# Four-layer scan network on one core: operand offsets, nine units of B on GpSimd placed by turn, Silus in the second turn, the line layer's addition one scan later

## The chip, the cores and the metric

The kernel runs on one NeuronCore of a Trainium2 chip. The metric is the time of one execution on the device, in microseconds (us). A core has five engines that run their own instruction streams and meet at semaphores: PE (TensorE, matrix products), DVE (VectorE), ACT (ScalarE), POOL (GpSimd) and SP, which here does nothing but issue DMAs. SBUF is the on-chip memory of 128 partitions, PSUM the smaller memory that PE writes and that DVE and ACT can read; DRAM tiles hold what is sent around.

## The reference, cut to what matters

Eight images of 48 x 48 pixels and 96 channels go through four residual layers, `x = x + layer(group_norm(x))`. Layers 0 and 3 are "SS2D" layers, layer 1 is a spectral layer (up-sampling, a small multi-layer product, low-pass), layer 2 is a line layer. Layers 0, 2 and 3 are selective scans. With u the convolved and Silu-activated input of 192 channels, 16 states and 4 directions:

```
xz = x @ in_proj;  u, z = split(xz);  u = silu(conv(u) + b)      # 3x3 in SS2D, 4 taps along the line in layer 2
x_dbl = u (in direction k) @ x_proj                              # -> dt (rank 6), B (16), C (16)
delta = softplus(dt @ dt_proj + bias)                            # one value per channel and pixel
for every pixel in the direction's order:
    h = h * exp(delta * A) + (delta * u) * B                     # h: 192 channels x 16 states
    y = sum over states of h * C
y = y + D * u
# SS2D: sum of the 4 directions over the whole image, layer norm, * silu(z), @ out_proj
# line layer: every row (or column) is its own sequence; * silu(z), @ outp, the directions joined by @ out_w
```

In SS2D one sequence runs through all 2304 pixels; in the line layer h starts anew in every row or column of 48 pixels.

## The kernel before, in words

**Tiling.** `scans` is the common body of layers 0, 2 and 3. A layer has 8 jobs (images) of 4 directions of 5 blocks: four blocks of 10 lines (480 columns) and one of 8 (384), 160 blocks in all. The 192 channels are two halves of 96, the 16 states and 96 channels of a half are folded into four groups of 128 partitions x 3 units. So a block has 8 slots (half and group, in the order of `ORDER`), each of three units of one block's columns, and four turns q of two slots (six units) each. A turn does, per pair of units, one scan on DVE (line 289) over both units at once. In the SS layers a unit has two more columns than the block (`m = n + 2`): at one side the state that came from the block before with `FAR` as its delta, at the other one that is multiplied by nothing; in the line layer `m = n`, and `FAR` is put on the first pixel of every line.

**What a turn computes, and where.** `make_da` (line 281): exp(delta * A) on ACT into one of two PSUM buffers, two exponentials for each scan. `make_dbu` (line 257): du * B into a room in SBUF, a part of the three units of a slot on DVE, with B from a PSUM copy that ACT makes (`copy_b`, line 238, one buffer), the rest on POOL, with B straight from the SBUF tile `bc`; `ON_POOL` says how many units of which slot are POOL's: seven in a block. `scan` runs in place in the room. `make_hc` (line 295): h * C on POOL, in place, eight times a block. `reduce` (lines 315, 317): sums over states on PE into PSUM, after an `opening` product that brings in what is summed so far (line 311). `done`: in SS a copy of y by ACT into the sum (line 671), in the line layer y * silu(z) on DVE (line 822), then two later steps, `project` on PE at +1 (line 831) and `add` on DVE at +2 (lines 837 and 839).

**What sets the order.** The schedule is by hand (`manual_schedule`): each engine runs its instructions in program order. The order within a turn t is that of the loop at line 368: scan(t,0); hc of the turn before; DVE's part of slot 2t+2; exponentials for the next scan; POOL's part of slot 2t+3; a reduction; scan(t,1); and so on. `aside` is called twice a turn, once a slot, and holds what stands beside the scans: the loads of B and C (`LOAD_BC`, slots 2, 3, 6, 7) and of delta and du (`LOAD_DD`, slots 4 and 5) for the next block, one step of the `side` generator, the steps of `stage1`, the `later` steps of `done`, and the `tail`.

**Stage 1** prepares block b + 2 while block b is scanned. In SS: slot 0 the product with x_proj on PE (line 630), slot 1 its copy `bcl` by ACT (line 635), slot 3 the store of B and C to DRAM and the first product for delta (line 620), slots 4 and 5 the biased copies (line 624), slot 6 Softplus on ACT (line 648), slots 7 and 8 du = delta * u on POOL (line 439), slots 9 and 10 `store_dd`, the stores of delta and du to DRAM (line 427). `load_dd` (line 212) and `load_bc` (line 224) read them back, broadcast over partitions. In the line layer stage 1 has the four-tap convolution on PE (line 759) in slots 3 and 4, its Silu `ub` (line 766) and the x_proj product (line 776) in slot 6, the copy `bcl` in slot 7, Softplus in slot 8, z and du in slot 9, the Silu of z `zb` (line 808) and the first store in slot 10, the second in slot 11. "Row" targets read a job's image by rows and "column" targets by columns, with strides.

**Beside the scans in SS** the `side` generator does, for each job, the end of the image before (`post`), the group norm of the next, and in the second half of the job the 3x3 convolution of the next image (`conv`): for each half of five blocks nine taps on PE spread over seven slots (line 501), with the gate's product z in the seventh, then a step with two Silus on ACT, u (line 510) and z (line 512). The convolution begins at step `10 * NG`, so that the Silus fall in slot 7. ACT loads another table for Silu, for Softplus and again for the exponentials (lines 281, 510 and 648, 1283 ns each).

DMAs are all issued by SP in program order, and one that waits holds those behind it.

## Time and profile before

| | before |
|---|---|
| median of 3 runs | 19150.31 us (19148.47 to 19160.53) |
| the profiled execution's own time | 19152.15 us |
| its span, first to last instruction | 19150.3 us |
| TensorE clock granted, mean | 0.754 of full speed |
| DVE busy | 16643.8 us (87%) |
| POOL busy | 15110.6 us (79%) |
| PE busy | 15031.5 us (78%) |
| ACT busy | 14070.7 us (73%) |
| scans of layer 0 | 119 to 5829 us |
| layer 1 | about 5829 to 7260 us |
| scans of layer 2 | 7260 to 13278 us |
| scans of layer 3 | 13404 to 19121 us |

The profile is of one execution. A group line gives line, engine, operation, tiles written <- tiles read, shapes, count, then busy time and mean duration (ns) of one, then the idle time of the engine just before such instructions and what ended most of it. A line of the waits gives engine and line, what was waited for, the total, the times and the longest. A line of the timeline gives start, duration, engine, line, operation and in brackets the idle time before it. "ps_" names are PSUM tiles.

### The profile page before, as it was taken

To read this page: it belongs to the slowest core of one execution; us is meant where nothing else is said; L and a number is where in the kernel's file an instruction comes from. 1 tells how busy PE (TensorE), PEld (TensorE's weight loads), DVE (VectorE), ACT (ScalarE), POOL (GpSimd) and SP (SyncE) were. 2 spreads that over 40 slices of the span, in tenths; PEclk is the share of its full clock that TensorE was granted. 3 is DMA by queue.
4 is the path that set the end of the run, shared out by engine and by line. 5 is a ranking of instruction groups with operands and counts; after the bars stand their busy time and mean duration, and the time that the engine had idled before them with its cause. 6 is when DMAs were issued, how large, how long until landed. Compare 5 with 4: busy or idle time off the path is not lost.

```text
span 19150.3 us, 170303 instructions
## 1 busy us (share of the span) xinstructions
PE 15031.5 (78%) x53500; PEld 4344.3 (23%) x53500; DVE 16643.8 (87%) x11289; ACT 14070.7 (73%) x20982; POOL 15110.6 (79%) x8304
## 2 busy tenths in 40 slices
PE   6777777777777997888888888887677777777776
PEld 1211211211214562222222222222121121121121
DVE  7999999999993227999999999997999999999998
ACT  6777877877872227888888888886778778778776
POOL 6899999899891006777777777776898998999998
PEclk7776776776767777887888888888777677677676
DMA  4444444444443324444444444443444444444444
GB/s 136 166 160 162 165 162 165 164 164 163 159 169 61 48 44 141 152 145 150 149 146 151 143 152 149 144 150 123 161 165 158 165 165 158 165 165 161 163 163 143
DMA packets 768469, 2831.72 MB, mean 148 GB/s; under 512 B 235724, under 2 KB 298668, under 8 KB 640926
## 3 DMA queue, kind: packets, MB, share of 16 engines
q1 hardware_dynamic: 767558, 2820.84, 44.7%
q8 instruction: 418, 6.85, 0.2%
q14 instruction: 493, 4.04, 0.1%
HBM read 2373.39 MB, written 447.18 MB: 147 GB/s over the span
## 4 chain that ended last, share of the span: by engine, by line
DVE 26%; PE 22%; ACT 18%; issue 16%; POOL 13%; DMA 4%; SPq 0%; DVEq 0%; POOLq 0%; ACTq 0%
DVE dbu L289 15%; POOL dbu L295 10%; DVE dbu L257 10%; PE ps_s L759 5%; ACT ps_da L281 5%; ACT L281 4%; PE ps_y L315 3%; PE ps_h L989 2%; POOL dbu L257 2%; PE ps_side L501 2%; PE ps_y L1002 2%; PE ps_s L831 1%; PE ps_s L630 1%; DMA dd<-dd 1%; DMA dd<-dds 1%
## 5 line engine op out<-in xcount | busy, mean ns | idle before, releaser
L289 DVE TENSOR_TENSOR_SCAN dbu<-ps_da,dbu 128x964 f32<-128x964 f32 (+3 forms) x5760 | 11863.3, 2072 | 884.6 <-ACT ps_da L281 862.4
L295 POOL TENSOR_TENSOR dbu<-dbu,bc 128x1440 f32<-128x1440 f32 (+1 forms) x3840 | 10685.9, 2796 | 2290.8 <-DVE dbu L289 2202.6
L281 ACT ACTIVATE ps_da<-dd,w_l_a 128x482 f32<-128x482 f32 (+3 forms) x11520 | 7428.3, 648 | 2851.4 <-DVE dbu L289 2636.8
L315 PE MATMUL ps_y<-dbu,w_red 128*32 128x480 f32 (+1 forms) x23040 | 4910.5, 745 | 2690.4 <-POOL dbu L295 2684.9
L317 PE MATMUL ps_y<-dbu,w_red 128*32 128x480 f32 (+1 forms) x7680 | 4869.1, 745 | 0.0
L257 DVE TENSOR_TENSOR dbu<-dd,ps_b 128x1443 f32<-128x1443 f32 (+10 forms) x3840 | 4414.3, 1150 | 264.6 <-ACT ps_b L238 217.0
L257 POOL TENSOR_TENSOR dbu<-dd,bc 128x962 f32<-128x962 f32 (+6 forms) x1920 | 3101.7, 1615 | 79.6 <-DMA dd<-dd 39.7
L315 PEld LDWEIGHTS ps_y<-dbu,w_red 128*32 128x32 f32 x23040 | 757.2, 126 | 6562.2 <-POOL dbu L295 4864.9
L238 ACT COPY ps_b<-bc 128x482 f32<-128x482 f32 (+3 forms) x3360 | 1805.0, 537 | 319.2 <-DVE dbu L257 288.5
L759 PE MATMUL ps_s<-xpad,w_l_cw 128*128 128x480 f32 (+1 forms) x2560 | 1758.4, 840 | 2.3 <-ACT xpad L142 1.6
L501 PE MATMUL ps_side<-xpad,w_l_cw 128*128 128x480 f32 (+1 forms) x2880 | 1604.8, 685 | 4.5 <-ACT xpad L142 4.5
L281 ACT ACT_TABLE_LOAD x986 | 1265.0, 1283 | 17.6
L131 POOL MEMSET w_l_cw<- 128x1760 f32 (+1 forms) x3 | 5.8, 1941 | 1340.3 <-DVE x L969 1334.9
L439 POOL TENSOR_TENSOR dds<-dds,u 96x480 f32<-96x480 f32 (+1 forms) x640 | 815.1, 1274 | 199.7 <-ACT dds L648 199.7
L630 PE MATMUL ps_s<-u,w_l_xp 96*38 96x480 f32 (+1 forms) x1280 | 932.7, 869 | 2.8 <-ACT dds L624 1.5
L620 PE MATMUL ps_s<-bcl,dtw 6*96 6x480 f32 (+1 forms) x1280 | 837.9, 742 | 108.1 <-ACT dds L624 99.8
L311 PE MATMUL ps_y<-ysum,w_ident 96*96 96x480 f32 (+1 forms) x960 | 753.2, 875 | 118.2 <-ACT ysum L671 118.1
L501 PEld LDWEIGHTS ps_side<-xpad,w_l_cw 128*128 128x128 f32 x2880 | 567.5, 222 | 1119.5 <-issue 907.5
L759 PEld LDWEIGHTS ps_s<-xpad,w_l_cw 128*128 128x128 f32 x2560 | 524.0, 210 | 1085.0 <-issue 999.6
L317 PEld LDWEIGHTS ps_y<-dbu,w_red 128*32 128x32 f32 x7680 | 697.3, 126 | 0.0
L776 PE MATMUL ps_s<-ub,w_l_xp 96*38 96x480 f32 (+1 forms) x640 | 382.7, 734 | 245.8 <-ACT ub L766 245.8
L800 PE MATMUL ps_s<-xpad,w_l_inz 96*96 96x480 f32 (+1 forms) x640 | 494.0, 904 | 97.6 <-ACT dds L794 80.9
(146 smaller groups left out, 11996.1 us busy)
## 6 DMA issues: line engine op xcount, KB each, us to landing
dd<-dd SPq DMA_DIRECT2D x512, 1446.0 KB
bc<-bcd SPq DMA_DIRECT2D x1536, 480.0 KB
dd<-dd SPq DMA_DIRECT2D x256, 1440.0 KB
dd<-dds SPq DMA_DIRECT2D x512, 361.5 KB
dd<-dd SPq DMA_DIRECT2D x128, 1158.0 KB
bc<-bcd SPq DMA_DIRECT2D x384, 384.0 KB
dd<-dds SPq DMA_DIRECT2D x256, 360.0 KB
dd<-dd SPq DMA_DIRECT2D x64, 1152.0 KB
```

Source lines behind the costliest of these rows:

```text
L238: nc.scalar.copy(bps[t][:, :b.m], bcs[t][0])
L257: engine.tensor_mul(o, du, by.unsqueeze(1).to_broadcast([P, hi - lo, by.shape[1]]))
L281: nc.scalar.activation(da[:, at:at + b.m], b.got[half][:, u % 3, 0, :], AF.Exp, scale=a[:, b.k, ci:ci + 1])
L289: nc.vector.tensor_tensor_scan(db, da, db, 0.0, ALU.mult, ALU.add)
L295: nc.gpsimd.tensor_mul(h, h, bcs.pop(2 * t + sub)[1].unsqueeze(1).to_broadcast([P, 3, n]))
L315: nc.tensor.matmul(y[32 * g:32 * g + 32, :n], lhsT=wc["red"][:, :32], rhs=hc[:, g, b.at], start=False, stop=(slot == 3))
L317: nc.tensor.matmul(y[DH:, :n], lhsT=wc["red"][:, 32:], rhs=hc[:, 2, b.at], start=(slot == 0), stop=(slot == 3))
L439: nc.gpsimd.tensor_mul(rows(du, n), rows(dt, n), u)
L501: nc.tensor.matmul(pu[:, :n], lhsT=flat[:, at:at + P], rhs=xpad[:, r0 + dy:r0 + dy + nr, dx:dx + W], start=(tap == 0), stop=(tap == 8))
L620: nc.tensor.matmul(got["p"][:DH, :n], lhsT=dtw[2 * NS:, b.k, half, :], rhs=b.bcl[2 * NS:, :n], start=True, stop=True)
L630: nc.tensor.matmul(got["p"][:NBC, :n], lhsT=w[f"{l}_xp"][:, b.k, half, :], rhs=u[:, half], start=(half == 0), stop=(half == 1))
L759: nc.tensor.matmul(got["u", half][:, :n], lhsT=flat[:, at:at + P], rhs=shifted(off), start=(tap == 0), stop=(tap == 3))
```

## The change

1. Operand offsets: a unit of the SS layers has four columns more than the block (was two), so the scans have 968 columns (were 964); the tiles `bc`, `dds` and `zin` begin their data two elements in (`LEAD = 2`; `bc` began at one, the others at nought), and `dds` is laid out by half, then delta and du, with a helper `make_room`. The rooms are set to zero once a layer.
2. `ON_POOL` becomes two tables of nine units: one for SS, one for the line layer. Where all three units of a slot are on POOL, ACT makes no copy of B for it. POOL's part of slot 2t+2, which was empty, is issued in turn t as well.
3. `LOAD_DD` goes from slots 4 and 5 to 3 and 5. In SS both du products are made in slot 7, and the two stores go to slots 8 and 9 (were 9 and 10).
4. In SS the convolution begins five steps earlier, which puts the two Silus into slot 2, in the second turn; the gate's product is put behind the other work of its slot (`tail`).
5. In the line layer `add` goes from +2 to +3, and steps above +2 are run inside the turn, right after DVE's part of slot 2t+2 and before the second scan (`early`).

```diff
@@ -24,11 +24,13 @@
 BMAX = 480
-WMAX = BMAX + 2
+WMAX = BMAX + 4
+LEAD = 2
 NG = 8
 LOAD_BC = (2, 3, 6, 7)
-LOAD_DD = (4, 5)
+LOAD_DD = (3, 5)
 NBUF = 6
@@ -37,7 +39,9 @@
 CH = 96
-ON_POOL = {1: 1, 3: 2, 5: 2, 7: 2}
+ON_POOL_SS = {2: 1, 3: 3, 5: 1, 6: 1, 7: 3}
+ON_POOL_L2 = {3: 2, 5: 1, 6: 3, 7: 3}
 DIRS_SS = [(False, False), (True, False), (False, True), (True, True)]
@@ -74,9 +78,9 @@
             return
-        self.m = self.n + 2
+        self.m = self.n + 4
         self.at = slice(1, self.n + 1)
-        self.came, self.goes = (self.m - 1, 0) if self.back else (0, self.m - 1)
+        self.came, self.goes = (self.n + 1, 0) if self.back else (0, self.n + 1)
         self.by = slice(0, self.n + 1) if self.back else slice(1, self.n + 2)
...
@@ -199,11 +204,13 @@
         rooms = [pools["dbu"].tile([P, 6 * WMAX], F32, tag="dbu", name="dbu") for _ in range(NG // 2)]
-        bufs = [pools["bc"].tile([P, 1 + 2 * BMAX], F32, tag=f"bc{n}", name=f"bc{n}") for n in range(NBUF)]
+        bufs = [pools["bc"].tile([P, LEAD + 2 * BMAX], F32, tag=f"bc{n}", name=f"bc{n}") for n in range(NBUF)]
         for buf in bufs:
-            nc.gpsimd.memset(buf[:, 0:1], 0.0)
+            nc.gpsimd.memset(buf[:, :LEAD], 0.0)
+        for room in rooms:
+            nc.gpsimd.memset(room, 0.0)
         dbus, das, bps, bcs, ys = {}, {}, {}, {}, {}
-        later, ends = {}, []
+        later, early, ends = {}, {}, []
         free = {n: 0 for n in range(NBUF)}
@@ -221,21 +228,23 @@
             rows4 = b.bcd[8 * sg:8 * sg + 8, :].rearrange("(s w) n -> s (w n)", w=2)
-            nc.sync.dma_start(r[:, 1:1 + 2 * b.n], rows4.unsqueeze(0).to_broadcast([32, 4, 2 * b.n]))
-
-            lead = b.at.start
-            bcs[t] = bcs[other] = r[:, 1 - lead:1 - lead + b.m], r[:, 1 + b.n:1 + 2 * b.n]
+            nc.sync.dma_start(r[:, LEAD:LEAD + 2 * b.n], rows4.unsqueeze(0).to_broadcast([32, 4, 2 * b.n]))
+            lo, hi = LEAD - b.at.start, LEAD + b.n
+            bcs[t] = bcs[other] = r[:, lo:hi + b.at.start], r[:, hi:hi + b.n]
         def copy_b(t):
             b, slot = blocks[t // NG], t % NG
-            if slot == NG // 2:
+            if on_pool.get(slot) == 3:
+                return
+            if slot == NG // 2 and t - 1 in bps:
                 bps[t] = bps[t - 1]
             bps[t] = ps("b", 1)
-            nc.scalar.copy(bps[t][:, :b.m], bcs[t][0])
+            nc.scalar.copy(bps[t][:, :bcs[t][0].shape[1]], bcs[t][0])
         def units(tile, b, lo, hi):
@@ -247,7 +256,7 @@
                 dbus[t // 2] = rooms[t // 2 % (NG // 2)]
-            cut = 3 - ON_POOL.get(slot, 0)
+            cut = 3 - on_pool.get(slot, 0)
             lo, hi = (0, cut) if engine is nc.vector else (cut, 3)
@@ -298,7 +307,7 @@
                 for n, step in done(b, half, ys.pop((b, half))):
-                    later.setdefault(at + n, []).append(step)
+                    (early if n > 2 else later).setdefault(at + n, []).append(step)
         def reduce(t, sub):
@@ -376,7 +385,10 @@
             make_dbu(at + 2, nc.vector)
+            for step in early.pop(at, []):
+                step()
             make_da(t, 1)
+            make_dbu(at + 2, nc.gpsimd)
             make_dbu(at + 3, nc.gpsimd)
...
@@ -424,12 +436,15 @@
     def store_dd(b, half):
-        nc.sync.dma_start(b.dd[half].rearrange("j (g m) -> g j m", g=3), b.dds[:, half, :2 * b.m])
+        nc.sync.dma_start(b.dd[half].rearrange("j (g m) -> g j m", g=3), b.dds[:, half].rearrange("p t m -> p (t m)"))
     def sizes(b, half):
-        t = b.dds[:, half]
-        return [t[:, n * b.m:(n + 1) * b.m][:, b.at] for n in range(2)]
+        return [b.dds[:, half, n, b.at] for n in range(2)]
+    def make_room(b, pools):
+        b.room = pools["dds"].tile([DH, LEAD + 4 * WMAX], F32, tag="dds", name="dds")
+        b.dds = b.room[:, LEAD:LEAD + 4 * b.m].rearrange("p (h t m) -> p h t m", h=2, t=2)
     def make_du(b, half, u):
@@ -441,9 +456,10 @@
         elif half == 0:
-            ends = b.dds[:, :, :2 * b.m].rearrange("p h (t m) -> p h t m", t=2)
-            nc.gpsimd.memset(ends[:, :, :, b.came:b.came + 1], FAR)
-            nc.gpsimd.memset(ends[:, :, :, b.goes:b.goes + 1], 0.0)
+            far = b.dds[:, :, :, b.came:] if b.back else b.room[:, :4 * b.m].rearrange("p (u m) -> p u m", m=b.m)[:, :, :LEAD + 1]
+            nc.gpsimd.memset(b.dds[:, :, :, 0:1] if b.back else b.dds[:, :, :, b.goes:], 0.0)
+            nc.gpsimd.memset(far, FAR)
     def ss2d(l, xin, xout, b0=0):
@@ -486,7 +502,7 @@
             nc.sync.dma_start(xpad[:C, 1:1 + H, 1:1 + W], seq(xin[b], False))
-        def conv(b, blks):
+        def conv(b, blks, behind=lambda step: step()):
             if blks[0] == BLKS[0]:
@@ -502,14 +518,18 @@
                         if slot == 6:
-                            pz = ps("s1", 1)
-                            nc.tensor.matmul(pz[:DH, :n], lhsT=w[f"{l}_in"][:, (2 + half) * DH:(3 + half) * DH],
-                                             rhs=xpad[:C, 1 + r0:1 + r0 + nr, 1:1 + W], start=True, stop=True)
+                            got = {}
+                            def gate():
+                                got["z"] = ps("s1", 1)
+                                nc.tensor.matmul(got["z"][:DH, :n], lhsT=w[f"{l}_in"][:, (2 + half) * DH:(3 + half) * DH],
+                                                 rhs=xpad[:C, 1 + r0:1 + r0 + nr, 1:1 + W], start=True, stop=True)
+                            behind(gate)
                         yield
                     z = zp.tile([DH, BMAX], F32, tag="z", name="z")
-                    nc.scalar.activation(z[:, :n], pz[:DH, :n], AF.Silu)
+                    nc.scalar.activation(z[:, :n], got["z"][:DH, :n], AF.Silu)
                     yield
@@ -546,8 +566,9 @@
                 s = slice(r0 * W, r0 * W + n)
-                z = lnp.tile([DH, 2, BMAX], F32, tag="zin", name="zin", bufs=1)
-                nc.sync.dma_start(z[:, :, :n], zs[b][:, :, s])
+                z = lnp.tile([DH, LEAD + 2 * BMAX], F32, tag="zin", name="zin", bufs=1)
+                z = z[:, LEAD:LEAD + 2 * n].rearrange("p (h n) -> p h n", h=2)
+                nc.sync.dma_start(z, zs[b][:, :, s])
                 xi = xio.tile([C, BMAX], F32, tag="xi", name="xi")
@@ -560,7 +581,7 @@
                 yield
-                nc.gpsimd.tensor_mul(y[:, :, s], y[:, :, s], z[:, :, :n])
+                nc.gpsimd.tensor_mul(y[:, :, s], y[:, :, s], z)
                 po = side_psum()
@@ -595,10 +616,11 @@
                     yield
-                while used < 10 * NG:
+                while used < 10 * NG - 5:
                     used += 1
                     yield
-                yield from conv(job + 1, BLKS)
+                yield from conv(job + 1, BLKS, tail.append)
             else:
@@ -639,22 +661,23 @@
             def s4():
-                b.dds = pools["dds"].tile([DH, 2, 2 * WMAX], F32, tag="dds", name="dds")
+                make_room(b, pools)
                 biased(0)
             def s6():
-                both = b.dds[:, :, b.at]
+                both = b.dds[:, :, 0, b.at]
                 nc.scalar.activation(both, both, AF.Softplus)
-            def du(half):
-                return lambda: make_du(b, half, u[:, half])
+            def du():
+                for half in range(2):
+                    make_du(b, half, u[:, half])
             def store(half):
                 return lambda: store_dd(b, half)
-            return {0: s0, 1: s1, 3: s3, 4: s4, 5: lambda: biased(1), 6: s6, 7: du(0), 8: du(1),
-                    NG + 1: store(0), NG + 2: store(1)}
+            return {0: s0, 1: s1, 3: s3, 4: s4, 5: lambda: biased(1), 6: s6, 7: du,
+                    NG: store(0), NG + 1: store(1)}
         def so_far(b, half):
@@ -671,13 +694,13 @@
             return []
-        dirs = DIRS_SS
+        dirs, tail = DIRS_SS, []
         load_x(0)
             pass
-        scans(dirs, (0, 1, 3, 2), False, a, pools, ps, stage1, opening, done, side, [])
+        scans(dirs, (0, 1, 3, 2), False, ON_POOL_SS, a, pools, ps, stage1, opening, done, side, tail)
         for _ in post(nb - 1, BLKS[:1]):
@@ -789,7 +812,7 @@
                 nc.sync.dma_start(b.bcd, b.bcl[:2 * NS, :n])
-                b.dds = pools["dds"].tile([DH, 2, 2 * WMAX], F32, tag="dds", name="dds")
+                make_room(b, pools)
                 for half in range(2):
@@ -840,7 +863,7 @@
                     nc.sync.dma_start(xout[b.job], xs[b.job])
-            return [(1, project), (2, add)]
+            return [(1, project), (3, add)]
         def side(job):
...
```

More of the change, by code (lines that the diff above doesn't have):

```diff
@@ L181, in norm_scale, with scans @@
         yield
-    def scans(dirs, order, restart, a, pools, ps, stage1, opening, done, side, tail):
+    def scans(dirs, order, restart, on_pool, a, pools, ps, stage1, opening, done, side, tail):
         blocks = [Block(job, k, blk, n == 0, n == len(BLKS) - 1, dirs[k][1])
@@ L404, in scans @@
         finish(2 * nt)
-        while later:
-            for step in later.pop(min(later)):
+        for n in sorted([*later, *early]):
+            for step in later.pop(n, []) + early.pop(n, []):
                 step()
@@ L858, in lines @@
             pass
-        scans(dirs, range(NK), True, a, pools, ps, stage1, opening, done, side, tail)
+        scans(dirs, range(NK), True, ON_POOL_L2, a, pools, ps, stage1, opening, done, side, tail)
         stack.close()
```

## The prediction

> **What bounds the kernel now.** I read the page's busy table and its chain first, then the same engines by stage, the groups by form in one stage, the waits, and the timeline of a few blocks. The stage table (us; then PE, PE weight loads, DVE, ACT, POOL busy with counts, TensorE clock, DMA share, GB/s) for the scans of layer 0, of the line layer and of layer 3:
>
> ```profile
> 119.00:5829.00 5710.00, 4281.90 (x15204) 1083.44 (x15204) 5383.31 (x3494) 4410.10 (x6647) 5159.63 (x2842) 0.71 0.48 162
> 7260.00:13278.00 6018.00, 5127.93 (x15956) 1340.47 (x15956) 5556.10 (x3767) 4886.27 (x7073) 4734.23 (x2553) 0.83 0.42 147
> 13404.00:19121.00 5717.00, 4245.57 (x15204) 1072.80 (x15204) 5391.06 (x3494) 4410.27 (x6647) 5160.41 (x2843) 0.72 0.48 162
> ```
>
> These three stages are 17,445 of 19,150 us. DVE is busy 94% of the first and third and 92% of the second: it sets the pace, POOL stands 4 points behind it in the outer two, and PE (75%) runs at a clock of 0.71. The page's chain says that the pace is handed round, not DVE's alone:
>
> ```profile
> DVE 26%; PE 22%; ACT 18%; issue 16%; POOL 13%; DMA 4%; SPq 0%; DVEq 0%; POOLq 0%; ACTq 0%
> ```
>
> The groups by form, first of layer 0 between 800 and 5600 us (the L289 line is the scan, L257 the products with B, L295 the products with C):
>
> ```profile
> L289 DVE TENSOR_TENSOR_SCAN dbu<-ps_da,dbu 128x964 f32<-128x964 f32 x1292 | 2759.2, 2153 | 164.5 <-ACT ps_da L281 155.8 <-issue 5.2 <-POOL dbu L295 3.4
> L295 POOL TENSOR_TENSOR dbu<-dbu,bc 128x1440 f32<-128x1440 f32 x862 | 2564.2, 2989 | 390.5 <-DVE dbu L289 388.7
> L257 DVE TENSOR_TENSOR dbu<-dd,ps_b 128x1443 f32<-128x1443 f32 x431 | 703.2, 1632 | 1.7 <-DMA dd<-dd 1.1 <-ACT ps_da L281 0.7
> L257 POOL TENSOR_TENSOR dbu<-dd,bc 128x962 f32<-128x962 f32 x323 | 610.3, 1890 | 0.0
> L257 DVE TENSOR_TENSOR dbu<-dd,ps_b 128x481 f32<-128x481 f32 x323 | 202.9, 628 | 0.0
> L257 DVE TENSOR_TENSOR dbu<-dd,ps_b 128x962 f32<-128x962 f32 x108 | 121.9, 1129 | 0.0
> L257 POOL TENSOR_TENSOR dbu<-dd,bc 128x481 f32<-128x481 f32 x108 | 111.9, 1036 | 0.0
> ```
>
> and of the line layer between 7700 and 12700:
>
> ```profile
> L295 POOL TENSOR_TENSOR dbu<-dbu,bc 128x1440 f32<-128x1440 f32 x852 | 2321.2, 2734 | 794.3 <-DVE dbu L289 724.3 <-DMA bc<-bcd 69.9
> ```
>
> The same 1440-element product takes 2989 ns in the SS layers and 2734 in the line layer: only the operands' offsets differ. DVE's idle time and the two waits that the change works on (engine, waited for, total, times, longest):
>
> ```profile
> DVE dbu L289 <- ACT ps_da L281: 862.4, 842, 3.8
> ACT bcl L635 <- PE ps_s L630: 422.0, 214, 5.8
> ```
>
> A scan waits for exponentials when ScalarE is held up; in the SS layers it is held up by table loads, and by the bcl copy (L635) that waits for PE. In layer 0's block from 2007.1 us:
>
> ```profile
> 2007.58 1.28 ACT L510 ACT_TABLE_LOAD   x1
> ...
> 2012.69 2.17 DVE L289 TENSOR_TENSOR_SCAN dbu<-ps_da,dbu 128x964 f32<-128x964 f32 x1 [1.87 <-ACT ps_da L281]
> 2012.84 0.50 PEld L501 LDWEIGHTS ps_side<-xpad,w_l_cw 128*128 128x128 f32 x2 [1.56 <-ACT ps_da L281]
> ...
> 2017.51 0.47 ACT L635 COPY bcl<-ps_s 38x384 f32<-38x384 f32 x1 [0.33 <-PE ps_s L630]
> ```
>
> The Silu pair's load costs DVE 1.87 us in turn 0; the turn thereby lengthens to 10 us, and the bcl copy, 10.4 us after the block's start, then delays nothing.
>
> **What the Trainium skill says.** "GPSIMD Engine Reference", 3.1 Elementwise, has about 2.6 cycles an element on GpSimd against 1 on DVE, and nothing of offsets; the trace's 1440 elements cost 2734 or 2989 ns on POOL and 1632 on DVE, the same order. "SBUF — State Buffer", Who interferes with whom, has DVE and GpSimd share a port pair under a lock; DVE reads B from PSUM here, and POOL's products keep their durations beside it, so I charge nothing. "ScalarE: Activation LUTs", What ACT_TABLE_LOAD costs, gives 1283 ns and a drain of 1380 more; the trace has the 1283 and the Silu 1.29 us after the load's start, so the measured 1.28 is used. "TensorE: Matmul & The Clock Gate", Part 1, lets PE fall to half speed after an idle window; granted clocks of 0.71 and 0.83 agree that PE is often slow, and I price PE by its slow records.
>
> **The change, part by part.** A block of 480 columns lasts on average 36.2 us in SS and about 38 in the line layer (160 blocks a layer, 32 of them with 384 columns, taken at 0.82 of the price).
>
> *Offsets.* If POOL's SS products fall to 2740 (the line layer's row), 8 x 0.25 = 2.0 us of POOL a block. POOL then pays for two more units. SS before: 8 x 2.99 + 1.04 + 3 x 1.89 + du 2 x 1.32 = 33.3; after: 8 x 2.74 + 3 x 1.04 + 2 x 2.74 + about 2.4 = 32.9. A three-unit product with B is in no row; I take 2.74 from the C product of that size, bounds 2.7 and 3.1. Without the offsets' effect it is 23.9 + 3.1 + 6.0 + 2.6 = 35.6, only 0.6 below a block. The scans grow from 964 to 968: from 772 (1753) to 964 (2153) an element is 2.08 ns, so 12 x 8 ns = +0.1 us a block in SS. The rooms' memsets come once a layer: under 10 us of POOL, beside loads of weights, nothing.
>
> *Units.* DVE's products with B before: 4 x 1632 + 1129 + 3 x 628 = 9545 ns in 8 instructions; after in SS: 3 x 1632 + 3 x 1129 = 8283 in 6, in the line layer 4 x 1629 + 1124 + 628 = 8268 in 6. Neighbouring DVE records overlap by some 0.083 us, so the gain is 1.26 - 0.17 = 1.09 us a block. In full it is 1.09 x (128 + 0.82 x 32) x 3 = 504, less 31 for the longer scans: -473. ScalarE loses one B copy of 0.55 us in SS and two in the line layer.
>
> *SS, Silus in the second turn.* In places 0 to 9 of a job (no convolution beside) DVE's gain should appear: -0.99 a block, -9.4 us a job, -75 a layer; job 7 has no convolution in its second half either, -9. In the 70 blocks with convolution DVE's own work falls from 33.7 to 32.75. Before, stalls of 2.4 made 36.1. Now turn 0 has three scans and one two-unit product: 7.3 us. Scan (1,1) is due at 7.3 + 2.07 + 1.55 = 10.9, and its two exponentials (1.33) and the bcl copy (0.5) stand ahead of it, so that the copy must start at 9.1. It needs the xp matmuls, which stand behind the last reduction (hc ends at 3.7, +1.75) and now behind two conv taps instead of one (a tap is 1.97 us in the block above): 10.4 + 1.9, less what the earlier hc gives, so 11.0 to 12.1. The stall is 1.9 to 3.0. The Silus in turn 1 put 2 x 1.28 + 0.66 + 0.55 = 3.77 between exponentials with two buffers of da, about 1.75 of it showing. That makes 36.4 to 37.5 instead of 36.1; with the column places I take +1.3, so 70 x 1.3 = +91 a layer. Each SS layer: -75 - 9 + 91 = about +7; two: +15. The moved gate matmul (0.9 us) only goes behind the other work of its slot. du in one step and stores a slot earlier take the slack of two slots; nobody waits.
>
> *Line layer.* Where targets are rows (12 places of 20) DVE and ACT allow 35.8 after 37.4 to 38: -1.75, bound 0 to -2. Where targets are columns (8 places) the round of PE work (z, project, a strided convolution of 8 x 0.94 us, ub, xp) holds at about 38 as before: 0. SP is one queue: load_dd(0) now comes a slot earlier, before store_dd(1), and waits for store(0) to land. In the block from 9182.4:
>
> ```profile
> 9192.35 0.73 SPq L427 DMA_DIRECT2D dd<-dds  x1
> 9193.13 0.53 SPq L224 DMA_DIRECT2D bc<-bcd  x1
> 9193.77 1.52 SPq L427 DMA_DIRECT2D dd<-dds  x1
> 9202.54 6.41 SPq L212 DMA_DIRECT2D dd<-dd  x2
> 9210.88 3.20 SPq L224 DMA_DIRECT2D bc<-bcd  x2
> ```
>
> store(1) goes at 11.4 and the load at 20.2. Held behind that load, store(1) goes after 20 and lands at 31 to 34, load(1) goes after it, and the last bc loads land at 37 to 40, which is where ScalarE copies them: a round of about 36.8 (35 to 39). Between 35.8 and 36.8 I take -1.25: 96 x 1.25 = -120. The addition at +3 moves 0.6 us of DVE from behind a late project to a place where it waits for nothing: in that sum.
>
> Total +15 - 120 = -105 against the profiled span of 19,150.3. Its run took 19,152.2 and the median is 19,150.3, so that no correction is needed: about 19,040.
>
> **The rivals.**
> 1. *The gain arrives everywhere* (18,690, 0.22): -473, if the bcl copy starts by 9.1 (a warm PE needs half of 1.97 for a tap) and store(1)'s delay is covered by the earlier load. For it: DVE at 94%; against: the 422 us that the bcl copy already waits.
> 2. *Slower by the bcl copy* (19,300, 0.30): one mechanism, scan (1,1) behind the copy behind PE. If the copy starts at 13 the stall is 3.9, a convolution block is 32.75 + 1.75 + 3.9 = 38.4, so +2.3: 70 x 2.3 - 84 = +77 a layer, +154; the line layer at its loop's 38 gives nothing back. Above about 12.8 it cancels the line layer's -120. For it: clock 0.71; against: hc ends earlier with a quicker POOL.
> 3. *The offsets do nothing* (19,150, 0.12): POOL at 35.6 a block is as slow as DVE was, and gains and stalls cancel. Against it: two rows of 2989 and 2734 for one form.
>
> **How the numbers follow.** The forecast has 0.36, its own range 18,950 to 19,110. The range for 8 in 10 is 18,690 to 19,330: from rival 1 to a little beyond rival 2. A measurement of this kernel tells about 0.2%, 38 us, from no change. Forecast and rival 1, less the forecast's edge at 19,110, give faster 0.56; rival 2 slower, with a small part of rival 3, 0.31; the rest 0.13 the same.
>
> **What would show it.** L295 in SS near 2740 ns (else rival 3). DVE's L257 busy down by 1.26 us a block, and fewer of ScalarE's B copies. The wait of bcl on PE rising well above 422 us, and DVE's wait on ps_da not falling in SS. In the line layer row places at 36 to 37 us, column places unchanged, store(1) issued about 20 us into a block. If SS blocks beside the convolution come at 35 us, the forecast is too high by up to 350; if line blocks exceed 38, too low.

## The result

The changed kernel took 19,285.2 us (median of 4 runs, 19,283.0 to 19,288.7) against 19,155.4 before: a ratio of 1.0067, 95% interval 1.005 to 1.0085. The forecast was 19,040 and faster. The time lies inside the stated range (18,690 to 19,330), but on the other side of no change: a small gain was forecast, and a small loss came.

The spans differ by 132.1 us (19,282.4 less 19,150.3). From the first scan to the last, layer 0 grew from 5710.1 to 5753.9 us, the line layer from 6018.5 to 6069.7 and layer 3 from 5716.4 to 5754.3. The spectral layer (-5) and the gap behind the line layer (+5) cancel. So 44 + 51 + 38 us came from the three scan stages; +7, -120 and +7 had been forecast. Their table after, with the columns as before (us; PE, PE weight loads, DVE, ACT, POOL busy with counts; TensorE clock, DMA share, GB/s):

```profile
120.00:5874.00 5754.00, 4194.02 (x15203) 1061.74 (x15204) 5254.10 (x3174) 4299.13 (x6487) 5114.37 (x3001) 0.74 0.48 161
7299.00:13369.00 6070.00, 5084.44 (x15948) 1358.32 (x15948) 5409.13 (x3447) 4719.99 (x6754) 4957.74 (x2554) 0.83 0.42 146
13500.00:19254.00 5754.00, 4166.59 (x15203) 1061.11 (x15204) 5253.82 (x3174) 4299.32 (x6486) 5114.26 (x3000) 0.75 0.48 161
```

DVE did lose work: 5383 to 5254 us in layer 0, 5556 to 5409 in the line layer. The stages got longer all the same, so DVE's idle time grew by 173 us in the one and by 199 in the other. The parts' prices had been right, as the groups by form between 800 and 5600 us of layer 0 show:

```profile
L298 DVE TENSOR_TENSOR_SCAN dbu<-ps_da,dbu 128x968 f32<-128x968 f32 x1276 | 2719.6, 2160 | 220.3 <-ACT ps_da L290 215.0 <-POOL dds L462 1.6 <-POOL dbu L304 1.6
L304 POOL TENSOR_TENSOR dbu<-dbu,bc 128x1440 f32<-128x1440 f32 x852 | 2321.9, 2737 | 390.3 <-DVE dbu L298 367.4 <-DMA zin<-zd 12.9 <-DMA bc<-bcd 5.9
L266 POOL TENSOR_TENSOR dbu<-dd,bc 128x1443 f32<-128x1443 f32 x212 | 581.5, 2743 | 0.0
L266 DVE TENSOR_TENSOR dbu<-dd,ps_b 128x1443 f32<-128x1443 f32 x319 | 520.5, 1632 | 0.0
L266 DVE TENSOR_TENSOR dbu<-dd,ps_b 128x962 f32<-128x962 f32 x320 | 361.9, 1131 | 0.0
```

POOL's product with C fell from 2989 to 2737 ns (2740 forecast), the three-unit product with B costs 2743 (2740). What was lost is in the waits (engine, waited for, total, times, longest):

```profile
DVE dbu L298 <- ACT ps_da L290: 1115.9, 810, 4.9
ACT bcl L657 <- PE ps_s L652: 907.8, 316, 6.2
ACT ps_b L247 <- DMA bc<-bcd: 286.1, 122, 11.3
```

The first was 862.4 us before, the second 422.0; the third is new among the larger ones. The chain that ended last now names POOL before DVE:

```profile
POOL 26%; PE 20%; DVE 16%; issue 14%; ACT 14%; DMA 10%; SPq 1%; POOLq 0%; DVEq 0%; ACTq 0%
```

Below, scan (q,p) is scan p of turn q of a block, both counted from 0, and a place is a block's number within its job, 0 to 19.

**Line layer.** SP's timeline of the block that starts at 9198.2 us and ends at 9238.3 (start, duration):

```profile
9208.91 0.74 SPq L439 DMA_DIRECT2D dd<-dds  x1
9209.70 0.54 SPq L231 DMA_DIRECT2D bc<-bcd  x1
9219.04 0.51 SPq L219 DMA_DIRECT2D dd<-dd  x1
9219.65 0.72 SPq L439 DMA_DIRECT2D dd<-dds  x1
9230.88 0.53 SPq L219 DMA_DIRECT2D dd<-dd  x1
9231.50 1.21 SPq L231 DMA_DIRECT2D bc<-bcd  x2
```

The second store (L439) goes out at 21.4 us into the block instead of 11.4, behind a load that waited for the first store. The second load goes at 32.7, and the last two loads of B and C right after it. By the trace's semaphore events these land at 40.4 and 41.6 us on average, in blocks that last 38.0 (places 1, 2, 7 and 16 to 18 of a job; before, they landed at 34.6 and 35.9, in blocks of 37.8). ScalarE's copy of B for the next block's third slot waits for them, and DVE's product after scan (0,0) behind it.

**SS layers.** The block of layer 0 that starts at 1984.57 us, beside the convolution, has one of the longest of these waits (some lines left out):

```profile
1983.80 1.46 POOL L454 TENSOR_TENSOR dds<-dds,u 96x480 f32<-96x480 f32 x1
...
1985.67 1.43 POOL L454 TENSOR_TENSOR dds<-dds,u 96x480 f32<-96x480 f32 x1
...
1987.06 2.74 POOL L304 TENSOR_TENSOR dbu<-dbu,bc 128x1440 f32<-128x1440 f32 x1
...
1991.61 3.57 PE L517 MATMUL ps_side<-xpad,w_l_cw 128*128 128x480 f32 x4
...
1995.11 3.41 PE L652 MATMUL ps_s<-u,w_l_xp 96*38 96x480 f32 x4
1998.56 0.55 ACT L657 COPY bcl<-ps_s 38x480 f32<-38x480 f32 x1 [5.83 <-PE ps_s L652]
...
2000.48 2.17 DVE L298 TENSOR_TENSOR_SCAN dbu<-ps_da,dbu 128x968 f32<-128x968 f32 x1 [4.93 <-ACT ps_da L290]
```

It reads as a chain. Two du products stand on POOL ahead of the product with C, which ends 5.2 us into the block. The reductions wait for it, then come two taps of the convolution (3.57 us), then the product with x_proj, "xp" (3.41). The bcl copy starts at 14.0, and DVE has stood for 4.93 us before scan (1,1). On average over the places 11 to 14 the copy starts at 11.9 and DVE stands for 2.8 us.

### The profile page after: what moved, and what is told of

It is laid out like the page before. It is cut to its first block, busy times and chain, and to the rows that moved or that the text cites. A ratio compares the mean times of both kernels' runs of the same rounds, so it can differ in the third digit from the quotient of the medians.

```text
span 19282.4 us, 169908 instructions
## 1 busy us (share of the span) xinstructions
PE 14824.8 (77%) x53500; PEld 4327.2 (22%) x53500; DVE 16231.7 (84%) x10329; ACT 13682.8 (71%) x20342; POOL 15272.7 (79%) x8636
## 4 chain that ended last, share of the span: by engine, by line
POOL 26%; PE 20%; DVE 16%; issue 14%; ACT 14%; DMA 10%; SPq 1%; POOLq 0%; DVEq 0%; ACTq 0%
POOL dbu L304 19%; DVE dbu L298 10%; ACT ps_da L290 6%; DVE dbu L266 5%; DMA bc<-bcd 5%; POOL dbu L266 4%; DMA dd<-dds 3%; PE ps_s L652 3%; PE ps_y L324 3%; PE ps_side L517 3%; PE ps_s L782 2%; POOL dds L454 2%; ACT L290 2%; PE ps_h L1012 2%; PE ps_y L1025 2%
## 5 line engine op out<-in xcount | busy, mean ns | idle before, releaser
L298 DVE TENSOR_TENSOR_SCAN dbu<-ps_da,dbu 128x968 f32<-128x968 f32 (+3 forms) x5760 | 11830.6, 2076 | 1231.6 <-ACT ps_da L290 1115.9
L304 POOL TENSOR_TENSOR dbu<-dbu,bc 128x1440 f32<-128x1440 f32 (+1 forms) x3840 | 10079.4, 2635 | 2115.9 <-DVE dbu L298 2063.8
L290 ACT ACTIVATE ps_da<-dd,w_l_a 128x484 f32<-128x484 f32 (+3 forms) x11520 | 7414.4, 649 | 2790.4 <-DVE dbu L298 2568.6
L266 DVE TENSOR_TENSOR dbu<-dd,ps_b 128x962 f32<-128x962 f32 (+5 forms) x2880 | 3833.7, 1331 | 355.1 <-ACT ps_b L247 325.6
L266 POOL TENSOR_TENSOR dbu<-dd,bc 128x481 f32<-128x481 f32 (+5 forms) x2240 | 3913.5, 1762 | 205.8 <-DMA bc<-bcd 120.2
L247 ACT COPY ps_b<-bc 128x482 f32<-128x482 f32 (+3 forms) x2720 | 1450.3, 533 | 388.7 <-DMA bc<-bcd 286.1
L642 PE MATMUL ps_s<-bcl,dtw 6*96 6x480 f32 (+1 forms) x1280 | 778.0, 692 | 131.7 <-ACT dds L646 98.4
L652 PE MATMUL ps_s<-u,w_l_xp 96*38 96x480 f32 (+1 forms) x1280 | 873.8, 817 | 2.8 <-ACT dds L646 1.5
L657 ACT COPY bcl<-ps_s 38x480 f32<-38x480 f32 (+1 forms) x320 | 171.9, 537 | 907.8 <-PE ps_s L652 907.8
L810 PE MATMUL ps_s<-bcl,dtw 6*96 6x480 f32 (+1 forms) x640 | 434.4, 816 | 416.2 <-ACT bcl L804 416.2
```

Source lines behind the costliest of these rows:

```text
L247: nc.scalar.copy(bps[t][:, :bcs[t][0].shape[1]], bcs[t][0])
L266: engine.tensor_mul(o, du, by.unsqueeze(1).to_broadcast([P, hi - lo, by.shape[1]]))
L290: nc.scalar.activation(da[:, at:at + b.m], b.got[half][:, u % 3, 0, :], AF.Exp, scale=a[:, b.k, ci:ci + 1])
L298: nc.vector.tensor_tensor_scan(db, da, db, 0.0, ALU.mult, ALU.add)
L304: nc.gpsimd.tensor_mul(h, h, bcs.pop(2 * t + sub)[1].unsqueeze(1).to_broadcast([P, 3, n]))
L642: nc.tensor.matmul(got["p"][:DH, :n], lhsT=dtw[2 * NS:, b.k, half, :], rhs=b.bcl[2 * NS:, :n], start=True, stop=True)
```

## The experiments

Times are medians. Ratios are to the kernel before, run on the same chip beside them; its median there was 19,135 to 19,155 us. The differences in the text are between medians: by the ratios, the gains over the changed kernel are 13 to 25 us smaller, and those over the combined kernel up to 20 us larger.

| kernel | us | ratio, 95% interval |
|---|---|---|
| changed | 19,285 | 1.0067 (1.005 to 1.0085) |
| line loads in slots 4, 5 | 19,133 | 0.9996 (0.9987 to 1.0005) |
| taps out of slot 0 | 18,977 | 0.9913 (0.9899 to 0.9928) |
| Silus in slot 7 | 19,108 | 0.9982 (0.9974 to 0.999) |
| offsets only | 19,108 | 0.998 (0.9972 to 0.9988) |
| norm with scalars | 19,161 | 1.0013 (1.0005 to 1.0022) |
| combined (line loads, taps, norm) | 18,719 | 0.9782 (0.9768 to 0.9797) |
| offsets and units, no moves | 18,850 | 0.9853 (0.9836 to 0.9869) |
| B and C one element in | 20,055 | 1.0479 (1.0464 to 1.0495) |
| Silus in slot 7, du in 7 and 8 | 19,044 | 0.9948 (0.9934 to 0.9963) |
| combined, addition at +2 | 18,711 | 0.9776 (0.9761 to 0.979) |
| no moves, norm, taps | 18,728 | 0.9784 (0.9769 to 0.9798) |
| combined, du in 7 and 8 | 18,604 | 0.9714 (0.9699 to 0.9728) |
| combined, SS loads in 4, 5 | 18,715 | 0.977 (0.9755 to 0.9784) |
| combined, du and stores back | 18,536 | 0.9681 (0.9664 to 0.9697) |
| combined, du, stores, SS loads back | 18,536 | 0.9681 (0.9665 to 0.9697) |

**The line layer's loads back in slots 4 and 5.**

```diff
+        load_dds = (4, 5) if restart else LOAD_DD
...
-                if slot in LOAD_DD:
-                    load_dd(blocks[nblk], LOAD_DD.index(slot))
+                if slot in load_dds:
+                    load_dd(blocks[nblk], load_dds.index(slot))
```

> The changed kernel, with the line layer's two loads of delta and du back in slots 4 and 5 (SS keeps 3 and 5). Theory, SP's queue: the first load in slot 3 stands ahead of the second store and holds it for some 10 us, so the last two loads of B and C land after the block's end and ScalarE's copy of B, and DVE's product behind it, wait for them. Then DVE's idle time before the product after scan (0,0) in the line layer (about 126 us) goes, its second store is issued near 11 us into a block again, its scans take 5940 to 6000 us after 6070, and the whole 19,160 to 19,220. Rival, the units' places: turns without DVE units are short and the gated product waits for PE; then the line layer stays above 6040 and the whole above 19,250.

Only the first load of each block moves, by one slot. The whole fell by 152 us to 19,133, more than expected. The stage table's line for the line layer:

```profile
7286.00:13210.00 5924.00, 5088.77 (x15952) 1344.45 (x15956) 5385.09 (x3447) 4722.54 (x6755) 4950.33 (x2554) 0.83 0.42 150
```

5924 us, 146 less than changed and 94 less than before; the SS layers stayed at 5755 and 5754. DVE's idle time before the product after scan (0,0) fell from 108 us to nothing, and its wait for the gated product after scan (0,2) from 64 to 12; that before the gated product after scan (2,2) stayed (111 and 109), and one before the product after scan (3,0), for the load of du, came up (2 to 100; 41 in the kernel before). The rival's waits exist, but they are not the loss. The early load in SP's queue is, and it cost more than the layer lost: without it the line layer gains.

**Taps out of slot 0 (SS).**

```diff
-                        for tap in ((0,), (1, 2), (3,), (4, 5), (6,), (7, 8), ())[slot]:
+                        for tap in ((0,), (1, 2), (3,), (4, 5), (6, 7), (), (8,))[slot]:
```

> The changed kernel, with the nine taps of the SS convolution shared out so that slot 0 has none and slot 1 one (the two that stood in slot 0 ahead of the xp products go elsewhere). Theory, PE's queue: the bcl copy is late because the xp products stand behind two taps; then it comes some 3 us earlier, DVE's idle time before scan (1,1) in places 9 to 19 falls from about 205 us a layer to 60 or less, and the whole is 19,000 to 19,120. Rival, the reductions and xp alone are late enough, or the stall moves on to the Silus: the whole stays above 19,200.

-308 us, more than expected: 5601 us in each SS layer after 5754. The same two waits as above, over the whole kernel:

```profile
DVE dbu L298 <- ACT ps_da L290: 786.8, 762, 4.0
...
ACT bcl L657 <- PE ps_s L652: 551.3, 291, 6.2
```

On average over places 11 to 14 of a job (here and below, the numbers in brackets: 16 to 19) the bcl copy starts at 9.3 us (8.1) into a block instead of 11.9 (10.8). DVE's idle time before scan (1,1) in places 9 to 19 of layer 3 fell from 205 to 64 us, that before (2,0) from 113 to 82: the stall did not move on to the Silus.

**Silus back in slot 7.** The edit is `while used < 10 * NG` for `10 * NG - 5`.

> The changed kernel, with the SS convolution beginning at step 80 again, so that the Silus fall in slot 7. Theory, Silus in the second turn are what SS lost: the stalls before scans (1,1) and (2,0), about 205 and 105 us a layer, mostly go, and those before (0,0) and (0,1), some 190 us a layer in the kernel before, come back: 40 to 80 us less in each SS layer, the whole 19,130 to 19,210. Rival, the stall follows the table loads wherever they are: within 30 us of the changed kernel, 19,255 to 19,315.

19,108: -178 us, a little more than expected. The waits of places 9 to 19 changed places as the theory had it: (1,1) from 205 to 58, (2,0) from 113 to 0, and (0,1) from 0 to 149 (layer 3). With this alone the two SS layers (5669 and 5663) are already shorter than before (5710 and 5716).

**Offsets only.** The changed kernel with the maps of units, slots, Silus and addition of before.

> The changed kernel with only the first part of the change: offsets as changed, the units of B, the loads, the Silus and the addition as before. Theory, POOL does not set the pace: its products with C fall to 2740 ns in the SS layers, DVE's scans cost 15 us more a layer, and the whole is that of the kernel before, 19,120 to 19,190. Rival, POOL's late products held PE's reductions and the copies behind them: the whole is 100 us or more below before, under 19,055.

19,108, -0.2%, just below the expected span: cheaper POOL products by themselves are worth 20 to 25 us in an SS layer.

**Offsets and units, none of the moves.**

> The changed kernel without the moves: offsets and nine units of B as changed; the loads in slots 4 and 5, du and the stores in their slots, the Silus in slot 7 and the addition at +2 as before. Theory, the units themselves gain and the moves lost it: the line layer takes 5,930 to 6,000 us, an SS layer about 5,660 (the changed kernel with the Silus in slot 7 had 5,663 and 5,670), the whole 18,960 to 19,060. Rival, the nine units by turn cost what they save, and the moves only change where it is lost: 19,100 or more.

18,850, 1.5% faster than before and 435 us below the changed kernel; SS layers 5605 and 5610, line layer 5927. The nine units are a gain (some 250 us against the offsets only); the moves lost all of it. It was better than expected, so the Silus and the line loads, with 178 and 152 us, were not all of the loss.

**B and C one element in (SS).** The tiles `bc` begin at one instead of two, the rest as changed.

> The changed kernel, with the SS layers' tiles of B and C beginning one element in instead of two, which turns the distance between the operands of GpSimd's products with C by four bytes. Theory, that distance sets their duration: those of 1440 elements take 2950 to 3080 ns again in SS and 2737 in the line layer; GpSimd, 35 us a block then, holds DVE up where blocks take less, and the whole is 19,290 to 19,450. Rival, the distance is not what counts: 2737 ns and 19,285 within 30.

```profile
L305 POOL TENSOR_TENSOR dbu<-dbu,bc 128x1440 f32<-128x1440 f32 x810 | 2613.2, 3246 | 75.8 <-DVE dbu L299 70.3 <-DMA bc<-bcd 4.0 <-POOL dbu L305 0.2
```

3246 ns instead of 2737, from four bytes (and 3251 instead of 2743 for three units of B), and 20,055 us. Both are worse than expected. POOL hardly waits ahead of these products (75.8 us in 4800): it is the bound of the SS layers (6141 and 6140 us), while the line layer, whose tiles were left alone, stays at 6071. So nine units are lost if every product is a slow one. The layout of before was not as bad (2989 ns), and nine units were not run with it: that they need the new offsets, which with seven units are worth 0.2%, follows from the forecast's sum for POOL (35.6 us of a block of 36.2) and is not shown.

**The group norm's second operand.** Four DVE instructions of 96 values per image, such as

```diff
-        nc.vector.tensor_sub(dev, mv[:, 0:1], gm)
+        nc.vector.tensor_scalar(dev, mv[:, 0:1], gm, None, ALU.subtract)
-        nc.vector.scalar_tensor_tensor(shift, gm, -1.0, rs, ALU.mult, ALU.mult)
+        nc.vector.tensor_scalar(shift, gm, rs, -1.0, ALU.mult, ALU.mult)
```

What suggested it is the timeline of the changed kernel in layer 0:

```profile
1102.99 2.75 POOL L266 TENSOR_TENSOR dbu<-dd,bc 128x1443 f32<-128x1443 f32 x1
...
1104.44 1.31 DVE L171 TENSOR_TENSOR dev<-mv,gm 96x1 f32<-96x1 f32 x1
1105.69 2.74 POOL L304 TENSOR_TENSOR dbu<-dbu,bc 128x1440 f32<-128x1440 f32 x1
1105.78 2.66 DVE L172 TENSOR_TENSOR dev<-dev 96x1 f32<-96x1 f32 x1
1108.47 0.15 DVE L173 TENSOR_TENSOR dev<-dev,mv 96x1 f32<-96x1 f32 x1
```

Each of the first two DVE instructions ends when POOL's ends (POOL's end, then DVE's: 1105.74 and 1105.75; 1108.43 and 1108.44). The third runs beside an idle POOL.

> The changed kernel, with the four small DVE instructions of the group norm (96 values each) written so that the second operand is a scalar per partition and not a second SBUF tensor. They take 64.6 us in layer 0, 27.8 in layer 2 and 65.2 in layer 3, though 155 ns is enough for one when GpSimd is idle; in the trace they end within 16 ns of the end of a GpSimd instruction. Theory, a DVE instruction with two SBUF tensors waits until GpSimd's running instruction ends: all fall to about 150 ns, and the whole by 100 to 145 us less what other work then waits, 19,140 to 19,200. Rival, they wait for something else or the scalar operand waits as well: durations stay, the whole is 19,260 to 19,310.

The groups of the kernel before between 800 and 5600 us:

```profile
L179 DVE SCALAR_TENSOR_TENSOR shift<-gm,rs 96x1 f32<-96x1 f32 x6 | 14.5, 2410 | 0.2
L168 DVE TENSOR_TENSOR dev<-dev 96x1 f32<-96x1 f32 x6 | 0.9, 155 | 0.2
```

of the changed kernel:

```profile
L183 DVE SCALAR_TENSOR_TENSOR shift<-gm,rs 96x1 f32<-96x1 f32 x6 | 33.7, 5612 | 0.2
L172 DVE TENSOR_TENSOR dev<-dev 96x1 f32<-96x1 f32 x6 | 15.9, 2656 | 0.2
```

and of the one with scalars:

```profile
L183 DVE TENSOR_SCALAR shift<-gm,rs 96x1 f32<-96x1 f32 x6 | 1.3, 210 | 0.2
L172 DVE TENSOR_SCALAR dev<-dev 96x1 f32<-96x1 f32 x6 | 1.3, 210 | 0.2
```

210 ns for all of them, and -124 us in the whole. Before the change the four took 37.8 us in layer 0, after it 64.6 (in the three scan layers together 108 and 157): POOL is found at work more often. So they took 27 us more in a layer that grew by 44. Most of what the scalars gain was there to be had before the change; at most some 49 us of it belong to the change.

**The three together.**

> The changed kernel with the line layer's loads in slots 4 and 5, the SS taps shared out without slot 0, and the group norm's scalars. Theory, three separate causes in different stages: the gains add, -152 (loads, measured) -308 (taps, measured) and that of the norm, up to -140: 18,690 to 18,830. Rival, they overlap: the gain of one hides that of the other, 18,900 to 18,980.

18,719: the gains add (152 + 308 + 124 = 584; 566 measured; by the ratios 534 and 546). They are three separate causes.

**du in two slots, with the Silus in slot 7.**

> The changed kernel with the Silus in slot 7 and, in SS, du of the two halves in slots 7 and 8 again (the stores stay in slots 8 and 9). The kernel with the Silus in slot 7 alone takes 5,663 to 5,670 us in an SS layer, the one with all moves undone 5,605 to 5,610. Theory, two du products one behind the other (2.9 us of GpSimd) ahead of the product with C delay a reduction and PE's steps behind it: most of those 55 us a layer go, the whole 18,990 to 19,030. Rival, the stores, the earlier load or the deferred gate product cost them: 19,080 to 19,130.

19,044: -63 us against the kernel with the Silus alone in slot 7, between the two expected spans. POOL's product with C ends at 2.9 us into a block of layer 3 instead of 4.4 (places 11 to 14; 3.5 in layer 0), with xp 1.7 us earlier.

**What the rest of the moves cost**, on the combined kernel. First the addition at +2:

> The combined kernel (loads in slots 4 and 5 in the line layer, SS taps out of slot 0, norm's scalars; 18,719 us, line layer 5,922) with the line layer's addition at +2 again. Theory, the late addition is worth its wait: before, DVE waited 74 us for the projection in the additions; these come back in part, the line layer takes 5,940 to 6,000, the whole 18,730 to 18,800. Rival, the place makes no difference: 18,719 within 20.

18,711: no difference; the theory's 20 to 80 us are not there, and the line layer takes 5924 us as before (5922). Then the kernel without moves, with norm's scalars and the taps shared out as ((), (0, 1), (2,), (3, 4), (5,), (6, 7), (8,)):

> The kernel without the moves (18,850 us) with norm's scalars and with the SS taps shared out so that slot 0 has none. Theory: norm is worth 60 us in an SS layer and some 10 in the line layer, the bcl copy's remaining waits little: 18,690 to 18,740. Rival, gains hide each other: above 18,770.

18,728, as expected. Then the combined kernel with du in slots 7 and 8, the stores in 9 and 10 and the loads in 4 and 5:

> The combined kernel (18,719 us) with du in slots 7 and 8, the stores in slots 9 and 10 and the loads in slots 4 and 5 in SS too, so that of the moves only the Silus in the second turn and the addition stay. Theory, the du products in one slot cost here as well: 30 to 55 us less in each SS layer, 18,610 to 18,670. Rival, with the taps out of the way they cost nothing: 18,719 within 25.

18,536, far below: 99 and 89 us less in the SS layers. Its parts, one by one:

> The combined kernel (18,719 us) with only du of the two halves in slots 7 and 8 in SS again. Theory, the second du product ahead of GpSimd's product with C is the whole cost of that part: like the kernel with du, stores and loads all put back, 18,520 to 18,570. Rival, half of it as in the kernel with the Silus in slot 7 (there 63 us): 18,640 to 18,680, and the rest is SP's order of stores and loads.

> The combined kernel with only the SS loads of delta and du in slots 4 and 5 again. Theory, GpSimd's du products are the whole cost: 18,719 within 25. Rival, the load in slot 3 holds SP's queue in SS too: 18,620 to 18,680.

> The combined kernel with du in slots 7 and 8 and the stores in slots 9 and 10 in SS again, the loads left in slots 3 and 5. Theory, the place of the stores is of no account: the same as with du alone put back, within 20 us. Rival, later stores behind a load in slot 3 are held in SP's queue as in the line layer: 40 us or more slower than with du alone; or earlier stores cost: 40 us or more faster.

du alone gives 18,604 (-115, between its two expected spans), du and stores 18,536 (-183), the loads alone 18,715 (nothing clear of the noise). So the du products in one slot cost some 60 us a layer here. With du alone put back, the bcl copy of layer 0 starts at 8.0 us (7.6) instead of 9.3 (7.9) beside the convolution, and place 6, where DVE waits for `post`'s product, takes 37.3 us instead of 39.3. The stores' 68 us are less clear: 24 us in each SS layer of the profiles, and some 15 in the spectral layer, whose code is the same. Why a later store helps was not tried.

The last two kernels of the table are the best of all, 3.2% below before, and they keep the Silus in the second turn. The stages of the last:

```profile
119.00:5567.00 5448.00, 4243.01 (x15205) 1073.22 (x15206) 5193.89 (x3174) 4296.28 (x6487) 5100.72 (x3003) 0.73 0.50 170
7000.00:12927.00 5927.00, 5104.43 (x15952) 1347.36 (x15956) 5372.17 (x3447) 4721.73 (x6754) 4953.70 (x2554) 0.83 0.42 150
13055.00:18510.00 5455.00, 4252.38 (x15205) 1065.26 (x15205) 5194.40 (x3174) 4295.23 (x6487) 5100.49 (x3004) 0.73 0.50 170
```

Against the 18,728 of the nearest kernel with the Silus in slot 7 (which has the addition at +2 and other taps as well) it is 192 us faster. This speaks for the second turn as the place of the Silus once nothing delays the bcl copy; no run moved them alone in this kernel.

## Why the prediction was wrong

*Prices.* Right for the parts that the change touches: 2737 ns for the products with C, 2743 for three units of B, DVE's products with B 195 us less in layer 0 (the forecast's 1.26 us a block make 194), scans +7 ns each. (The sum for DVE's products before is 9541 ns, not 9545, which changes nothing.)

*SS, places with convolution.* Right in mechanism and nearly in size. The copy was forecast at 11.0 to 12.1 us with a stall of 1.9 to 3.0 us before scan (1,1) and 1.75 for the Silus. Measured were 11.9 in places 11 to 14 (10.8 in 16 to 19), stalls of 2.8 (1.7) and 1.5 (1.4). In the seven jobs with a convolution the second half grew by 9.3 us (351.8 to 361.1) where 13 were forecast.

*SS, places without convolution.* This step failed: DVE's gain "should appear" there, -9.4 us a job, and -2.2 came in layer 0 (360.9 to 358.7). Three things took it. Place 9 was counted as free, but the convolution that begins five steps earlier reaches into it (+2.0). The norm's small instructions took 3.8 us more a job. DVE waited longer for the products of `post`, the end of the image before: over the eight jobs of layer 3 together from 1.9 to 9.2 us in place 1 and from 16.4 to 21.7 in place 6.

*"du in one step and stores a slot earlier take the slack of two slots; nobody waits."* This step failed. POOL's product with C, PE's reductions and xp wait: the forecast took the end of that product ("hc") at 3.7 us or earlier, it was 4.5. The runs price du at 63 us (Silus in slot 7) to 115 (combined).

*"I charge nothing"* for the port that DVE and GpSimd share. Wrong in one place: it holds for the big products, of whose inputs one is in PSUM, but not for the norm's instructions with two SBUF tensors, which grew by some 49 us in the three layers. The Trainium skill's page "SBUF — State Buffer", Who interferes with whom, says that a DVE instruction with two SBUF inputs contends with a GpSimd instruction that reads SBUF, and that the one that comes second is blocked. The trace agrees (2656 ns beside GpSimd, 155 alone, 210 with scalars); the forecast looked only at the instructions that the change touches.

*Line layer.* This term decided the sign: -120 forecast, +51 measured, 171 of the 237 us between the forecast's sum (19,045) and the span (19,282). The mechanism was described, with its times: store at 20, landing at 31 to 34, last loads at 37 to 40 (measured 21.4, 32.6, and 40.4 and 41.6). The step that failed is the next one, "a round of about 36.8": a load that lands behind the end of a 38.0 us block cannot leave a round of 36.8, since ScalarE copies from it before the next block's second turn. The column places were held to be bound by PE alone, at 0; places 8 to 17, where the targets are columns (ten; the forecast took eight), lost 8.4 us a job, and the others gained 2.0 instead of the 15 forecast. The prediction named the sign of this: line blocks above 38 us; those of 480 columns took 38.2. With the loads back in slots 4 and 5 the layer gains 95 us, 10.3 us a job in the row places and 1.6 in the column ones. Then the forecast of columns nearly unchanged is met, and the row places with 480 columns take 37.0 on average.

*The rivals.* Rival 2 (19,300) came nearest in time. Its mechanism is in the trace, but not at its price: the copy came at 10.8 to 11.9 us, not 13, and it needed the line layer's loss beside it. Rival 1 (18,690) is what no run of the change by itself reached: the units without the moves gave 18,850, and 18,536 was measured only with the norm's scalars and the taps moved as well. That the measured time lies in the stated range is luck in part: of the loss the two SS layers gave 82 us, about half of rival 2's 154, and the line layer, where a gain was forecast, gave 51.

## What to carry to other kernels

Work taken from the busiest engine is only a gain if the others' order still meets the shorter turn: after such a change, read each wait that was hidden by the old length and ask what stands ahead of it in its own queue. In this queue a load that waits for a store belonged behind the store that SP could already send: one slot was worth 146 us. When a time for "lands" comes out behind the time for "needed", the gain is gone, and no average in between should be taken.

## What the runs showed of the hardware

The norm's DVE instructions with two SBUF tensors, when they met a running GpSimd instruction, ended only after the end of one, and not always of the first: 96 values took 2656 ns (the end of one) and 5612 ns (mostly of the fourth) beside GpSimd, 155 alone, and 210 always when the second operand was a scalar per partition. In the SS layers of the changed kernel they ended 9 to 56 ns after the end of a GpSimd instruction. With GpSimd at 3246 ns a product and hardly a gap between them, two of these took 8.5 and 10.2 us on average.

GpSimd's product of two fp32 tensors of 1440 elements took 2734 to 2737 or 3246 ns by nothing but where the operands begin: four bytes made the difference. Counted from the kernels' own layouts (and taking tiles to begin at a multiple of 16 bytes), the first operand lies 8 or 12 bytes from the second, modulo 16, wherever the product took 2734 to 2737, and 0 where it took 3246. The 2989 of the SS layers before is a mean of both. There the units lie 482 columns apart, so that of a turn's first slot two units stand at 0 and one at 8, of its second slot one at 0 and two at 8. Thirds of 3246 and 2737 give an estimate of 3076 and 2907 ns; over layer 0 of the kernel before the two slots took 3073 and 2907. In the block from 2007.1 us a second slot's product is the first of these lines, a first slot's the second:

```profile
2008.14 2.90 POOL L295 TENSOR_TENSOR dbu<-dbu,bc 128x1440 f32<-128x1440 f32 x1
2039.84 3.07 POOL L295 TENSOR_TENSOR dbu<-dbu,bc 128x1440 f32<-128x1440 f32 x1 [1.35 <-DVE dbu L289]
```
